# Layer-norm statistics in a Mamba, gated-linear-attention and soft-MoE stack: moved behind a step's scans and onto ScalarE, and into the last layer's loop

## The chip, the cores and the metric

The kernel runs on one core of a Trainium2 chip. A core has five engines that run at the same time, each through its own instruction queue in order: PE (TensorE, matrix products; PEld is its weight load), DVE (VectorE), ACT (ScalarE), POOL (GpSimd) and SP (SyncE, here only for starting DMAs). They wait for each other through semaphores. The metric is the device time of one execution in microseconds; less is better.

## The reference

The input is x of shape (4, 1024, 128), which is 4096 tokens of 128 numbers. Six layers are applied, each on a layer norm of x and each added back to x:

```python
x = x + 0.5 * moe(layernorm(x))        # 8 experts, top 2, capacity 1024
x = x + mamba(layernorm(x))            # 256 channels, 16 states, scan over 1024 steps
x = x + 0.5 * moe(layernorm(x))        # the same weights again
x = x + 0.5 * soft_moe(layernorm(x))   # 64 experts x 32 slots
x = x + gla(layernorm(x))              # gated linear attention, 16 heads of 8
x = x + 0.5 * soft_moe(layernorm(x))   # the same weights again
```

with

```python
def layernorm(x):
    m = mean(x, -1); v = var(x, -1)
    return (x - m) / sqrt(v + 1e-5)
```

In the Mamba layer, for every channel d and state n, `h[t] = exp(delta[t,d]*A[d,n]) * h[t-1] + delta[t,d]*B[t,n]*u[t,d]` and `y[t,d] = sum over n of h[t]*C[t,n]`; then `y = (y + u*D) * silu(z)` and the output is `y @ W_out`. In the soft layer, logits of tokens against 2048 slots are taken through a softmax within each expert (32 slots, to gather tokens into slots) and through one across experts (64, to give the slots' results back to the tokens).

## The kernel before, in words

x stays in on-chip memory all the time, as 32 tiles of 128 tokens x 128 numbers, all f32. Each of the six layer norms has three small arrays with one entry per token: mv (mean and variance), rstd and nmr. A tile is normalised by one ACT instruction, rstd * x + nmr (`ln_apply`, L156). What that needs is made in two parts. `ln_stats` takes, for a group of four tiles, a BATCH_NORM_STATS2 (L121) and a BATCH_NORM_AGGREGATE (L122) per tile on DVE, and one add of the epsilon to the variance (L125). `ln_root` raises the result to the power -1/2 on POOL (`ln_pow`, L135) and multiplies it with minus the mean on DVE (`ln_minus`, L142).

**The Mamba layer** handles four sequences in two halves of 512 tokens, one half after the other, and within a half 16 states; one state of one half is a step k of the loop. The order on each engine within the loop is that in which the code emits it (a manual schedule). A step k emits: the next instruction group of the finished half's `epilogue` (behind); `fetch` of the B and C rows for step k+3 (a DMA for ten of the 16 states, a PE broadcast, L658, for the other six; a DMA of C for four states at a time); `scan` of step k, two DVE scans of 512 tokens (L686); `keep`, on ACT, of the end state of a first half (L697); `decay` of step k+2, two ACT exponentials (L676); `times_c` of step k-1, the product hc of the state with C on POOL (L702); `feed` of step k+2, the product dBu, on POOL or on DVE (L668); `sums` of step k-2, four PE instructions that add hc into py (L717). Then come the next groups of the `prologue` of the coming half (normalisation, transposes L548, convolution L569, projections L575 and L587, Silu with table loads L580, and the softplus with DVE work at L627 to L631). hc has three buffers, dA four (two steps), the PE broadcast of B one.

A finished half's epilogue begins at step 2 of the next half: `zs` (L724, DVE) multiplies the gate with py, which `sums` of state 15 completes; two steps on, sixteen PE instructions make po (L730); one step on, DVE adds po to x (L736); one step on, `ln_stats` of the four tiles for the next layer norm.

**The second MoE layer** begins with the normalisation of all tiles (after `ln_root` over 16 tiles, twice) and with loads of the expert weights.

**The two soft layers** (`soft_bounded`) go in a first loop over 64 steps (32 tiles x 2 halves of the slots): logits on PE (L926), their minimum on DVE (L930), exponential on ACT (L935), sums of 32 and a reciprocal on DVE (L942, L943), a product on POOL (L947), a product with the tokens on PE (L958). In steps 0 to 3 of every eight, ACT normalises the next four tiles; in step 4 PE turns them (L912) and ACT takes them over (L917). The turn uses one of the two logits buffers. The second loop makes the exponentials the other way round (L1037, L1047), sums them on POOL (L1055) and mixes (L1071, L1081). In the first of these layers, `others` runs pieces of the MoE combination, with the layer norm's statistics, one piece per step of the first loop; in the last layer it is empty.

**The gated linear attention** (`gla_layer`) between them handles eight groups of 512 tokens with four steps each: PE spreads v (L1499), DVE multiplies with k (L1505) and scans (L1516), POOL multiplies with q (L1524), PE sums (L1538); an epilogue per group (L1547 to L1576) ends with an addition to x on DVE (L1576) and `ln_stats` of the group's four tiles for the last soft layer. After all eight, `ln_root` over 16 tiles runs twice. Work outside of a manual schedule is placed by the framework's planner.

Of the kernel before, what the change touches and what calls it, by code (L numbers as in the profile page):

```python
# [8 lines left out]
F32 = mybir.dt.float32  # L9
# [59 lines left out]
def macaron_kernel(ctx: ExitStack, tc: tile.TileContext, a: dict, out: bass.AP):  # L69
# [76 lines left out]
    def ln_root(ln, j0, n=4):  # L146
        ln_pow(ln, j0, n)
        ln_minus(ln, j0, n)

    def ln_group(ln, j0):  # L150
        ln_stats(ln, j0)
        ln_root(ln, j0)

    def ln_apply(dst, j, ln):
        _, rstd, nmr = ln
# [332 lines left out]
    def mamba_layer(ln, ln_next, first):  # L488
# [4 lines left out]
        with ExitStack() as s:  # L493
# [227 lines left out]
            def epilogue(r):  # L721

                zs = r["zs"]
                nc.vector.tensor_tensor(zs, zs, r["py"], ALU.mult)  # L724
                yield
                yield
                po = ps.tile([P, NJ, D], F32, name="po", tag="mm")
                for i in range(NJ):
                    for c in range(NC):
                        nc.tensor.matmul(  # L730
                            po[:, i, :], zs[:, c, i * P : (i + 1) * P], w_out[:, c, :],
                            start=(c == 0), stop=(c == NC - 1),
                        )
                yield
                jj = r["b"] * (S // P) + r["h"] * NJ
                nc.vector.tensor_tensor(  # L736
                    x[:, jj : jj + NJ, :], x[:, jj : jj + NJ, :], po, ALU.add
                )
                yield
                ln_stats(ln_next, jj, NJ)  # L740
                yield


# [8 lines left out]
            with tc.manual_schedule(engines=ENGINES):  # L752
                bring, pieces = first
                for j in range(0, 16, 4):
                    bring(j)
                run(pieces(0))


                others = (_ for j in range(4, NT, 4) for _ in pieces(j))
                for _ in prologue(*halves[0], rs[0], psa, "dA"):  # L760
                    for _ in range(3):
                        next(others, None)
                run(others)
                for k in range(3):
                    at(fetch, k)
                at(feed, 0)
                at(feed, 1)
                at(decay, 0)
                at(decay, 1)
                LEAD = 5  # L770
                ahead, old, behind = (iter(()) for _ in range(3))
                for k in range(-LEAD, len(units) + 7):
                    if k % DS == DS - LEAD and (k + LEAD) // DS + 1 < len(rs):
                        i = (k + LEAD) // DS + 1
                        old, ahead = ahead, prologue(*halves[i], rs[i])
                    if k < 0:
                        next(ahead, None)
                        continue
                    if k > DS and k % DS == 2:
                        behind = epilogue(rs[k // DS - 1])  # L780
                    next(behind, None)
                    at(fetch, k + 3)
                    at(scan, k)
                    at(keep, k)
                    at(decay, k + 2)
                    at(times_c, k - 1)
                    at(feed, k + 2)
                    at(sums, k - 2)
                    next(old, None)
                    next(ahead, None)  # L790
# [75 lines left out]
        nc.vector.tensor_copy(smod, sm0.unsqueeze(1).to_broadcast([P, 4, PS]))  # L866
        return smod

    def soft_bounded(phiN, phiM, pbc, ew, eb, tag, ln, first=None, after=None, last=False):

# [10 lines left out]
        with ExitStack() as s:  # L881
# [223 lines left out]
            with tc.manual_schedule(engines=ENGINES):  # L1105
# [6 lines left out]
                    norm(i)  # L1112
                turn(0)
                take(0)
                others = iter(())
                if first:
                    run(pieces(4))
                    others = (_ for j in range(8, NT, 4) for _ in pieces(j))
                for k in range(NK + CS * NB + XL + 3):
                    next(others, None)  # L1120
                    if k < NK:
# [262 lines left out]
    def gla_layer(ln, ln_next):  # L1384
        with ExitStack() as s:
# [158 lines left out]
            def epilogue(u):  # L1544
# [31 lines left out]
                nc.vector.tensor_tensor(  # L1576
                    x[:, u * NJ : (u + 1) * NJ, :], x[:, u * NJ : (u + 1) * NJ, :], py, ALU.add
                )
                ln_stats(ln_next, u * NJ)
                yield  # L1580


# [68 lines left out]
    def after(j):  # L1651
        ln_group(lns[4], j)
# [2 lines left out]
    with tc.If(bounded > 0) as cmp:  # L1655
        def soft(*a_, **k_):
            soft_bounded(phiN, phiM, pbc, ew, eb, *a_, **k_)
        with tc.tile_pool(name="yb", bufs=2) as yp:
            soft("a", lns[3], combine(yp, gates[1], lns[3]), after)
        behind_soft(soft)  # L1660
    with cmp.Else():
        def soft(*a_, **k_):
            soft_layer(phiN, ew, eb, *a_, **k_)
# [82 lines left out]
```

## Time and profile before

| | us |
|---|---|
| median of 3 runs (2297.42 to 2300.35) | 2300.21 |
| the profiled execution | 2299.02 |
| its span, first to last instruction | 2297.1 |
| Mamba loop (first to last scan) | 304 to 834 |
| first soft layer, first loop, about | 1096 to 1336 |
| GLA, about | 1613 to 1797 |
| last soft layer, first loop, about | 1801 to 2026 |
| statistics of one group in the Mamba on DVE (398.96 to 401.36) | 2.40 |
| BATCH_NORM_STATS2 / AGGREGATE, mean of 192 | 0.277 / 0.192 |
| pow of 4 / of 16 columns on POOL | 1.01 / 2.90 |

How to read the lines: "L686 DVE" is line 686 of the kernel before, on VectorE. A row of the timeline gives start (us from the span's start), duration, engine, line, operation, output<-input, size and count of instructions merged; in brackets stands the idle time of that engine just before it and what ended the wait. Rows of a table by stage give the window, its length, busy time (with count) of PE, PEld, DVE, ACT and POOL, the granted PE clock as a share of full speed, the share of the DMA engines and GB/s. PE's busy time holds modelled ends of pipelined products.

### The profile page before, as it was taken

Reading aid. Unit: us, or ns where it says so; the run is one execution under the profiler, and the core shown is the slowest. Engines: PE = TensorE matmul, PEld = TensorE weight load, DVE = VectorE, ACT = ScalarE, POOL = GpSimd, SP = SyncE. Lnnn points to the kernel's source line nnn. Section 1 sums busy time; section 2 is a strip of 40 time slices with the busy share of each in tenths; the row PEclk is TensorE's granted clock in tenths of the full one; section 3 lists DMA queues with packets and bytes.
Section 4 is the critical chain, followed back from the end, with each engine's and each line's share of the span. In section 5 each row is a group of like instructions: output and inputs, shape, how many; then the busy total and the mean of one; then the engine's idle time right before and its main releaser. Section 6 shows DMA issues by size and latency. Waiting matters only on the chain. (4 is left out here: it accounts for less than half of the span.)

```text
span 2297.1 us, 17954 instructions
## 1 busy us (share of the span) xinstructions
PE 1931.9 (84%) x5889; PEld 903.0 (39%) x5889; DVE 1418.5 (62%) x1947; ACT 928.1 (40%) x1453; POOL 1400.0 (61%) x904
## 2 busy tenths in 40 slices
PE   4688568888988855886899989998888899989998
PEld 3466223333333314554344444443232344434443
DVE  4311578888888955111788745556888677754444
ACT  3222365566655523222444334332543333334331
POOL 2677267888988961777455556664444455556663
PEclk9999778999989885898999999999987899999999
DMA  7111333233323332112100000000000000000000
GB/s 248 35 52 51 105 126 107 92 116 93 104 90 106 115 142 78 51 51 64 37 19 0 0 1 0 1 0 6 1 1 0 0 0 0 1 1 5 10 10 15
DMA packets 63677, 111.23 MB, mean 48 GB/s; under 512 B 7999, under 2 KB 41423, under 8 KB 58581
## 3 DMA queue, kind: packets, MB, share of 16 engines
q1 hardware_dynamic: 45062, 81.37, 10.8%
q0 software_dynamic: 8192, 16.79, 2.6%
q10 hardware_dynamic: 10322, 11.85, 1.6%
q8 instruction: 48, 0.79, 0.1%
q14 instruction: 53, 0.43, 0.1%
HBM read 90.53 MB, written 19.44 MB: 48 GB/s over the span
## 5 line engine op out<-in xcount | busy, mean ns | idle before, releaser
L947 POOL TENSOR_TENSOR dm<-ex,sm 128x1024 f32<-128x1024 f32 x128 | 247.6, 1935 | 214.5 <-DVE sm L943 117.7
L702 POOL TENSOR_TENSOR hc<-hst,Cs 128x1024 f32<-128x1024 f32 x128 | 289.2, 2271 | 77.2 <-DVE hst L686 73.6
L717 PE MATMUL py<-hc,ident 128*128 128x512 f32 x512 | 278.9, 676 | 46.0 <-POOL hc L702 46.0
L1055 POOL TENSOR_TENSOR acc<-acc,L 128x1024 f32<-128x1024 f32 x96 | 225.9, 2354 | 116.5 <-ACT L L1047 115.8
L1047 ACT ACTIVATE L<-pl,pbc 128x512 f32<-128x512 f32 x256 | 162.1, 684 | 284.0 <-PE pl L1037 273.5
L926 PE MATMUL l<-phiT,xT 128*128 128x512 f32 x512 | 247.1, 607 | 18.5 <-ACT ex L935 15.2
L935 ACT ACTIVATE ex<-l,nmh 128x1024 f32<-128x1024 f32 x128 | 142.7, 1115 | 287.7 <-DVE nmh L930 269.9
L1037 PE MATMUL pl<-xT,phiM 128*128 128x512 f32 x512 | 244.1, 601 | 0.0
L1081 PE MATMUL py<-L,yt 128*128 128x512 f32 x512 | 238.4, 593 | 4.4 <-DVE L L1071 4.4
L958 PE MATMUL px<-dm,xn 128*128 128x512 f32 x512 | 240.8, 593 | 1.1 <-POOL dm L947 1.1
L676 ACT ACTIVATE dA<-delta,A 128x512 f32<-128x512 f32 x256 | 179.2, 721 | 95.1 <-DVE hst L686 90.0
L930 DVE TENSOR_REDUCE nmh<-l 128x1 f32<-128x1024 f32 x128 | 156.5, 1223 | 87.9 <-PE l L926 87.1
L717 PEld LDWEIGHTS py<-hc,ident 128*128 128x128 f32 x512 | 97.4, 204 | 204.2 <-issue 115.2
L389 ACT ACTIVATE hT<-ph,cols 128x512 f32<-128x512 f32 x128 | 88.0, 687 | 214.6 <-PE ph L385 214.6
L668 POOL TENSOR_TENSOR dBu<-du,Bs 128x1024 f32<-128x1024 f32 x80 | 171.8, 2149 | 0.6 <-ACT dA L676 0.6
L686 DVE TENSOR_TENSOR_SCAN hst<-dA,carry,dBu 128x512 f32<-128x512 f32 x128 | 154.2, 1261 | 5.6 <-POOL dBu L668 5.6
L926 PEld LDWEIGHTS l<-phiT,xT 128*128 128x128 f32 x512 | 97.6, 194 | 149.8 <-issue 116.9
L942 DVE TENSOR_REDUCE sm<-ex 128x32 f32<-128x1024 f32 x128 | 154.7, 1209 | 0.0
L686 DVE TENSOR_TENSOR_SCAN hst<-dA,dBu 128x512 f32<-128x512 f32 x128 | 146.6, 1201 | 7.6 <-POOL dBu L668 7.5
L404 DVE TENSOR_TENSOR eo<-po,b 128x512 f32<-128x512 f32 x32 | 22.1, 692 | 207.4 <-PE po L399 207.4
L363 POOL DMA_INDIRECT y_d<-eo,dest x128 | 125.8, 982 | 35.6 <-issue 25.6
L1071 DVE TENSOR_TENSOR L<-L,rd 128x1024 f32<-128x1024 f32 x128 | 147.1, 1213 | 0.1
(248 smaller groups left out, 2976.2 us busy)
## 6 DMA issues: line engine op xcount, KB each, us to landing
Cs<-bc_d SPq DMA_DIRECT2D x32, 1024.0 KB, 4.7
Bs<-bc_d SPq DMA_DIRECT2D x80, 256.0 KB, 3.3
w<-in_w SPq DMA_DIRECT2D x4, 2048.0 KB
y<-y_d SPq DMA_DIRECT2D x32, 256.0 KB, 3.3
y_d<-zero SPq DMA_DIRECT2D x1, 4096.0 KB
ew<-in_ew ACTq DMA_DIRECT2D x1, 4096.0 KB
x<-in_x SPq DMA_DIRECT2D x8, 256.0 KB, 7.6
xn_da<-xn ACTq DMA_DIRECT2D x8, 256.0 KB, 6.9
```

The lines of the kernel that those rows point to most:

```text
L668: eng.tensor_tensor(dBu, r["du"], r.pop(("B", n)).unsqueeze(2).to_broadcast([P, HB, NC]), ALU.mult,)
L676: nc.scalar.activation(dA, r["delta"][:, :, c], AF.Exp, scale=A[:, c * DS + n : c * DS + n + 1],)
L686: nc.vector.tensor_tensor_scan(hst[:, :, c], r.pop(("dA", n, c)), dBu[:, :, c], 0.0 if h == 0 else carry[b][:, c, n : n + 1], ALU.mult, AL ...
L702: nc.gpsimd.tensor_tensor(hc, r.pop(("h", n)), Cs.unsqueeze(2).to_broadcast([P, HB, NC]), ALU.mult)
L717: nc.tensor.matmul(r["py"][:, c, :], ident, hc[:, :, c], start=False, stop=(n == DS - 1))
L926: nc.tensor.matmul(l[:, q * 512 : (q + 1) * 512], xT[:, j * P : (j + 1) * P], phiN[:, o : o + 512], start=True, stop=True,)
L947: nc.gpsimd.tensor_tensor(dms[k], exs.pop(k), sms.pop(k).unsqueeze(2).to_broadcast([P, NG, PS]), ALU.mult,)
L958: nc.tensor.matmul(px[hf * 2 + q], xns[j // 4][:, j % 4, :], dmf[:, q * 512 : (q + 1) * 512], start=(j == 0), stop=(j == NT - 1),)
L1037: nc.tensor.matmul(pl[:, i, :], phiM[:, (2 * c + i) * P : (2 * c + i + 1) * P], xT[:, t * TB : (t + 1) * TB], start=True, stop=True,)
L1047: nc.scalar.activation(L[:, i, :], pl[:, i, :], AF.Exp, bias=pbc[:, 2 * c + i : 2 * c + i + 1], scale=-1.0,)
L1055: nc.gpsimd.tensor_tensor(accs[t], accs[t], L, ALU.add)
L1081: nc.tensor.matmul(pys[t], yt[:, 2 * c + i, :], L[:, i, :], start=(c + i == 0), stop=(c == CS - 1 and i == 1),)
```

## The change

Three things change.

1. In the Mamba's loop, the finished half's next group is emitted after the step's scans, no longer at the step's head. Its statistics are made by `ln_stats_act`: four ACT Copy instructions that also accumulate the sum of a tile, one that scales the sums to minus the mean, four ACT Square instructions with that as bias that accumulate the squares, and one that scales these to the variance plus epsilon. They write a throw-away tile `junk`. The root of this layer norm is `ln_root_pool`: the pow and the multiplication with minus the mean are both on POOL.
2. In the GLA, only the first two groups (tiles 0 to 7) still have `ln_stats`, and one `ln_root` over these eight tiles follows.
3. The last soft layer takes the statistics of tiles 8 to 31 in its first loop, as `others`, in eight pieces per group of four tiles: in steps 1 and 2 of eight the statistics, in step 3 the pow, in step 5 the product.

The other branch (`cmp.Else`, another form of the soft layer that this input doesn't take) runs these pieces at once.

```diff
+    def ln_stats_act(ln, j0, n=4):
+        mv, rstd, nmr = ln
+        js = slice(j0, j0 + n)
+        junk = small.tile([P, D], F32, name="junk")
+        for j in range(j0, j0 + n):
+            nc.scalar.activation(junk, x[:, j, :], AF.Copy, accum_out=mv[:, j, 0:1])
+        nc.scalar.activation(nmr[:, js], mv[:, js, 0], AF.Copy, scale=-1.0 / D)
+        for j in range(j0, j0 + n):
+            nc.scalar.activation(
+                junk, x[:, j, :], AF.Square, bias=nmr[:, j : j + 1], accum_out=mv[:, j, 1:2]
+            )
+        nc.scalar.activation(
+            rstd[:, js], mv[:, js, 1], AF.Identity, bias=eps_t, scale=1.0 / D
+        )
+
+    def ln_root_pool(ln, j0, n=4):
+        _, rstd, nmr = ln
+        js = slice(j0, j0 + n)
+        nc.gpsimd.tensor_tensor(
+            rstd[:, js], rstd[:, js], half_t.to_broadcast([P, n]), ALU.pow
+        )
+        nc.gpsimd.tensor_tensor(nmr[:, js], nmr[:, js], rstd[:, js], ALU.mult)
+
+    def ln_pieces(ln, j):
+        yield
+        ln_sums(ln, j, 2)
+        yield
+        ln_sums(ln, j + 2, 2)
+        ln_eps(ln, j)
+        yield
+        ln_pow(ln, j)
+        yield
+        yield
+        ln_minus(ln, j)
+        yield
+        yield
+        yield
...
@@ mamba_layer, epilogue @@
-                ln_stats(ln_next, jj, NJ)
+                ln_stats_act(ln_next, jj, NJ)
...
@@ mamba_layer, loop @@
-                    next(behind, None)
                     at(fetch, k + 3)
                     at(scan, k)
+                    next(behind, None)
                     at(keep, k)
                     at(decay, k + 2)
...
@@ soft_bounded, before the first loop @@
-                others = iter(())
                 if first:
                     run(pieces(4))
-                    others = (_ for j in range(8, NT, 4) for _ in pieces(j))
+                else:
+                    pieces = rest
+                others = (_ for j in range(8, NT, 4) for _ in pieces(j))
...
@@ gla_layer, epilogue @@
-                ln_stats(ln_next, u * NJ)
+                if u < 2:
+                    ln_stats(ln_next, u * NJ)
...
     for j in range(0, NT, 16):
-        ln_root(lns[2], j, 16)
+        ln_root_pool(lns[2], j, 16)
...
     def behind_soft(soft):
         gla_layer(lns[4], lns[5])
-        for j in range(0, NT, 16):
-            ln_root(lns[5], j, 16)
-        soft("b", lns[5], last=True)
+        ln_root(lns[5], 0, 8)
+        soft("b", lns[5], rest=lambda j: ln_pieces(lns[5], j), last=True)
```

More of the change, by code (lines that the diff above doesn't have):

```diff
@@ L867, in group_sum, with soft_bounded @@
         return smod
-    def soft_bounded(phiN, phiM, pbc, ew, eb, tag, ln, first=None, after=None, last=False):
+    def soft_bounded(phiN, phiM, pbc, ew, eb, tag, ln, first=None, rest=None, after=None, last=False):
         TB = 512
@@ L1658, in macaron_kernel @@
         with tc.tile_pool(name="yb", bufs=2) as yp:
-            soft("a", lns[3], combine(yp, gates[1], lns[3]), after)
+            soft("a", lns[3], combine(yp, gates[1], lns[3]), after=after)
         behind_soft(soft)
@@ L1662, in soft @@
         def soft(*a_, **k_):
+            rest = k_.pop("rest", None)
+            if rest:
+                for j in range(8, NT, 4):
+                    run(rest(j))
             soft_layer(phiN, ew, eb, *a_, **k_)
```

## The prediction

> **What bounds the kernel now.** I read the page first (busy shares), then a table by stage, then the three stages that the change touches, instruction by instruction.
>
> ```profile
> PE 1931.9 (84%) x5889; PEld 903.0 (39%) x5889; DVE 1418.5 (62%) x1947; ACT 928.1 (40%) x1453; POOL 1400.0 (61%) x904
> ```
>
> ```profile
> 372.00:438.00 66.00, 57.07 (x128) 22.02 (x126) 56.59 (x52) 39.33 (x55) 54.83 (x26) 0.92 0.33 105
> 1637.00:1660.00 23.00, 20.08 (x84) 6.75 (x84) 21.85 (x29) 12.54 (x19) 12.31 (x6) 1.00 0.00 0
> 1830.00:1858.00 28.00, 27.63 (x68) 12.28 (x67) 21.57 (x24) 10.92 (x13) 14.96 (x8) 1.00 0.00 1
> ```
>
> The columns of the three rows below the page's line are the window, its length, busy us of PE, PEld, DVE, ACT and POOL, then clock, DMA share and GB/s. The whole-kernel 62% for DVE says little. In a Mamba half (first row) PE, DVE and POOL are each busy 83 to 86% and ACT 60%: none is the bound for the whole half, they take turns. In the GLA (second row) DVE is at 95%. In the soft layer's first loop (third row) PE is at 99% and DVE at 77%.
>
> How the turns go in one Mamba half, from the timeline:
>
> ```profile
> 385.07 1.22 DVE L724 TENSOR_TENSOR zs<-zs,py 128x1024 f32<-128x1024 f32 x1 [6.00 <-PE py L717]
> ...
> 395.99 0.69 DVE L736 TENSOR_TENSOR x<-x,po 128x512 f32<-128x512 f32 x1 [1.51 <-PE po L730]
> ...
> 400.66 0.79 DVE L125 TENSOR_SCALAR rstd<-mv 128x4 f32<-128x4 f32 x1
> ```
>
> ```profile
> 388.83 2.13 POOL L702 TENSOR_TENSOR hc<-hst,Cs 128x1024 f32<-128x1024 f32 x1 [4.69 <-DVE hst L686]
> ...
> 403.98 2.13 POOL L702 TENSOR_TENSOR hc<-hst,Cs 128x1024 f32<-128x1024 f32 x1 [2.56 <-DVE hst L686]
> ```
>
> I write scan(n), hc(n), sums(n) for state n of the half. DVE stands 6.00 us before zs, because zs needs the previous half's sums(15), and it stands there in front of scan(2); POOL then waits 4.69 us for scan(2) to make hc(2). Six of the eight zs have this wait (5.99 to 6.00 us), the one in the last half has none, the eighth lies behind the loop. The statistics (398.96 to 401.36, 2.40 us) stand in front of scan(6), and POOL waits 2.56 us for it. From hc(6) to 428 us POOL has no gap, and DVE waits for it (0.88 us at 418.71): there POOL is the bound.
>
> **The change, part by part.** The sum is made on the profiled execution: 2299.0 us, of which the span is 2297.1.
>
> *Mamba, pieces behind the scans.* scan(2) goes ahead of zs. Its inputs are there: dBu(2) left POOL at 377.6 and dA(2) and dA(3) ACT before 378.8, so it runs 379.0 to 381.5 within the old wait. zs does not move, since the end of its wait is PE's sums(15) at 385.03, behind the next half's convolution in PE's queue, and PE's order of instructions is the same in both programs. So scan(3) starts at 386.2 in place of 388.6: 2.4 us. The add L736 now follows scan(5); its 1.51 us wait for po shrinks to about 0.6.
>
> *Mamba, statistics on ScalarE.* DVE loses 2.40 us per half. DVE then runs scan(3), scan(4), dBu(6), scan(5) from 386.2 to 394.6, the add to 395.9, and ends scan(6) at 398.4 in place of 403.8: DVE is 5.4 us earlier. POOL can't take all of it. hc has three buffers, so hc(6) needs sums(3) done, and PE has no slack there: from 386.35 to 397.7 it runs back to back (sums(2) starts at 395.79), then a 1.1 us broadcast, then sums(3), which I put at an end of 400.2 to 400.5. hc(6) so starts at about 400.5, not 403.98: 3.5 us. The same walk through the half at 441 gives 468.5 against 471.86: 3.4 us. Behind it POOL is dense, so its lead is kept to the half's end, and DVE and ACT, which lead by more, follow.
>
> ACT gets eight accumulating activations and two short ones per half. None exists in this trace. Nearest rows: a scaled 128x128 Copy 389 ns (L454), a 128x128 with a bias pointer 365 ns (L1560), a 128x2 Copy 190 ns (L697), and a dependent pair (L620, L622) 0.04 us apart: 4 x 0.39 + 4 x 0.37 + 2 x 0.19 + 10 x 0.04 = 3.8 us. [...] Queued behind it on ACT are dA(8), and the copy of dbc, for which PE's delta product waits. With dA(7) out at 397.9 the pieces end at 401.7, dA(8) at 403.2, scan(8) at 405.0; DVE is ready for scan(8) at 402.0 and gets its first input at 402.5, so it loses half a microsecond, hidden: hc(8) stood at 412.35 and now stands at 408.9. This cover holds until the ten take about 7.3 us. [...] No table load is added.
>
> Seven halves have an epilogue behind them. Six gain 3.4; the last, without the zs wait and with one POOL wait of 0.47, gains 0.5: -20.9.
>
> *POOL's pow and product.* The pow over 16 columns (2.90 us) stands in half 4. Before, it lay in a hole: hc(6) came 5.09 us after hc(5) there, 4.56 in other even halves, so it cost 0.5. Now it stands behind dBu(9), in the dense stretch, with a product of some 0.2: +2.6. The second pair at the end is hidden: the tiles that need it are normalised after 874, and ACT's own chain there (statistics, a 1.90 us copy, four expert-bias issues in between: done near 854) lies under the wait for weights that holds ACT until 860.22. If those weights came earlier, up to 7 us would show. The expert-bias DMAs go out some 4 us later, but on the same queue behind a 4 MB load.
>
> *GLA.* Six of eight groups of statistics (1.8 us each, 10.9 in all) leave DVE. At 95% this looks like 10.9 us. But:
>
> ```profile
> 1663.40 0.63 ACT L1551 ACTIVATE sq<-og 128x512 f32<-128x512 f32 x1
> ...
> 1664.44 1.13 PE L1499 MATMUL pv<-qkv,spread_w 32*128 32x512 f32 x4
> ...
> 1665.68 1.23 DVE L1505 TENSOR_TENSOR pv<-pv,qkv 128x1024 f32<-128x1024 f32 x1
> ...
> 1787.59 0.68 DVE L1547 SCALAR_TENSOR_TENSOR og<-po,fg 128x512 f32<-128x512 f32 x1
> ```
>
> After a group at 1657.5 to 1659.3, DVE's second product from there (1665.68) starts 0.1 us after PE's 1664.44 matmuls end, and these wait on ACT's square, which stands behind a copy of PE's own result (ended 1663.42). PE has no gap from 1653.4 to 1662.8. So 1.8 us of DVE time turns into a wait for PE: nothing gained in the loop. At the end one counts: the 1787.59 line waits only for the statistics ahead of it, PE was done at 1786.0: -1.5. At the seam the first min-reduce (1804.78) stood behind a pow-and-multiply pair: -0.3. Ends for this part: 0 and -11. The clock is an unknown too: the granted clock is 1.00 in some GLA windows and 0.57 from 1751 to 1800. [...]
>
> *Last soft layer.* It takes six groups of statistics (0.8 us in each of two steps, then the eps add, a 1.0 us pow on POOL, a 0.1 us product). The first soft layer shows the price of such pieces:
>
> ```profile
> 1173.10 1.28 DVE L125 TENSOR_SCALAR rstd<-mv 128x4 f32<-128x4 f32 x1
> ...
> 1176.77 1.98 PE L926 MATMUL l<-phiT,xT 128*128 128x512 f32 x4 [1.65 <-ACT ex L935]
> ...
> 1817.88 1.98 PE L926 MATMUL l<-phiT,xT 128*128 128x512 f32 x4 [0.37 <-ACT ex L935]
> ```
>
> There the eps add stretched to 1.28 us beside POOL in the step that also turns a tile group, where both logits buffers are taken, and PE stood 1.28 us longer (1.65 against 0.37 without pieces): 7.7 us for six. In the new order the sums fall in steps 1 and 2 of 8 and the turn in step 4. DVE has 0.70 us spare per step: late by 0.1 after step 1, by at most 1.5 after step 2, and back to about 0 after step 4's reduce. So +0.3 in all, with 0 and +7.7 as ends.
>
> Sum: -20.9 + 2.6 - 1.5 - 0.3 + 0.3 = -19.8; 2299.0 becomes 2279.2. The runs' median is 2300.2, 1.2 above the profiled one: 2280.4, say **2280**.
>
> **Rivals.** A: *PE does not hold POOL back* (sums keep up because the hc arrive earlier), so DVE's 5.4 us pass on: 6 x 2.0 = 12 more, 2268; with part of the GLA's 10.9, down to 2258. Against it: PE's row of 57.07 in 66. B: *a part is given back*, by statistics of 7 to 9 us on ACT or by the soft layer's 7.7: 2287 to 2295. C: *PE sets the half's pace throughout*, and the change does not do what it says: DVE and POOL wait for sums later, only the 0.7 us that PE waits for ACT at 389.99 goes, 6 x 0.7 - 2.6 + 1.8: within 4 us, 2297. Against it: PE waits 2.3 us for POOL at 434.19, so it catches up within the half. D, *slower*: the accumulating activations are long. Between dA(7) and dA(8), each microsecond above 7.3 delays scan(8), then POOL, by one in seven halves; 3.5 us more eat the gain, so it decides from 10.8 us, or 1.25 us per activation, over three times the nearest row. At 1.6 us the ten take 13.6: 7 x 2.8 + 1 above, 2321.
>
> **How the numbers follow.** Likeliest 0.45 (its own range 2274 to 2287), A 0.17, B 0.18, C 0.09, D 0.11. The three runs before spread by 0.13%, so 0.2% (4.6 us) is about what a measurement tells from nothing. Faster: the likeliest, A and B, 0.80; same: C, 0.09; slower: D, 0.11. The range leaves out D, most of C and A's far end: 2262 to 2296.
>
> **What would show it.** Right: the wait before zs near 3.5 us, with scan(2) ahead of it; no POOL wait for scan(2); hc(6) 15.4 us after zs starts in place of 18.9; ten ACT pieces near 3.8 us in all; PE stalls of 0.4 us at the last layer's turns; GLA length less 1.5 only. Wrong: hc(n) waiting for PE more than I allow (C), a DVE wait for dA before scan(8) over 3 us (D), or GLA halves shorter than 19.3 us (A).

## The result, and the profile after

| | before | after |
|---|---|---|
| median | 2300.28 us (6 runs, 2297.42 to 2307.24) | 2275.64 us (6 runs, 2273.84 to 2278.42) |
| ratio after / before | | 0.9890, 95% interval 0.9875 to 0.9906 |
| the profiled execution, its span | 2299.02, 2297.1 us | 2274.64, 2272.9 us |

The kernel is faster by 1.1%, 24.6 us; 2280 was predicted. The lines of the two programs differ: 686 became 727 (scan), 702 became 743 (hc), 717 became 758 (sums), 724 became 765 (zs), 736 became 777 (the addition to x). I again write scan(n), hc(n) and sums(n). The page's busy shares of after, and three rows of its table by stage (window, length, busy us of PE, PEld, DVE, ACT, POOL, then clock, DMA share, GB/s), for the windows that answer to those shown before:

```profile
PE 1914.3 (84%) x5889; PEld 894.6 (39%) x5889; DVE 1404.0 (62%) x1878; ACT 954.6 (42%) x1597; POOL 1404.5 (62%) x911
```

```profile
371.26:437.26 66.00, 57.65 (x131) 22.20 (x130) 58.09 (x46) 44.22 (x76) 58.39 (x27) 0.94 0.34 105
1618.80:1641.80 23.00, 20.08 (x84) 6.74 (x84) 21.85 (x29) 12.49 (x19) 12.36 (x6) 1.00 0.00 0
1805.50:1833.50 28.00, 27.63 (x68) 12.25 (x67) 23.97 (x34) 10.91 (x13) 15.85 (x9) 1.00 0.00 1
```

In the Mamba half ACT has 4.9 us more, and POOL 3.6 us more in the same 66 us: POOL is fuller because it stands less. The GLA row in the middle of its loop is the same as before. The soft row has 2.4 us more of DVE and the same PE.

The sum by stage, from the starts of the same instructions in both traces:

| stage (us) | before | after | difference | predicted |
|---|---|---|---|---|
| start to the first zs | 385.07 | 384.33 | -0.74 | 0 |
| first zs to last zs (Mamba) | 454.94 | 437.24 | -17.70 | -18.3 |
| last zs to the GLA's first spread of v | 773.36 | 773.63 | +0.27 | 0 |
| that to the GLA's last addition to x | 183.22 | 174.63 | -8.59 | -1.5 |
| that to the first logits of the last soft layer | 4.34 | 4.34 | 0 | -0.3 |
| that to the last computing instruction | 492.12 | 494.17 | +2.05 | +0.3 |

The differences add up to -24.71; the two profiled executions differ by -24.38. The Mamba came out as forecast. Two small terms of the sum did not: the GLA gave 7.1 us more, and the last soft layer took 1.8 us more. The seam's -0.3 did not come either: the first minimum starts 3.82 us behind the first logits (3.85 before), because DVE now waits there for PE's logits.

The timeline of after, DVE and POOL at the head of the same half:

```profile
378.25 2.45 DVE L727 TENSOR_TENSOR_SCAN hst<-dA,carry,dBu 128x512 f32<-128x512 f32 x2
384.33 1.22 DVE L765 TENSOR_TENSOR zs<-zs,py 128x1024 f32<-128x1024 f32 x1 [3.64 <-PE py L758]
...
384.43 2.13 POOL L743 TENSOR_TENSOR hc<-hst,Cs 128x1024 f32<-128x1024 f32 x1 [1.00 <-POOL dBu L709]
...
389.53 2.13 POOL L743 TENSOR_TENSOR hc<-hst,Cs 128x1024 f32<-128x1024 f32 x1 [0.87 <-PE py L758]
393.43 2.14 POOL L743 TENSOR_TENSOR hc<-hst,Cs 128x1024 f32<-128x1024 f32 x1 [1.77 <-PE py L758]
...
400.06 2.13 POOL L743 TENSOR_TENSOR hc<-hst,Cs 128x1024 f32<-128x1024 f32 x1 [0.30 <-PE py L758]
...
403.09 4.81 DVE L727 TENSOR_TENSOR_SCAN hst<-dA,carry,dBu 128x512 f32<-128x512 f32 x4 [1.43 <-ACT dA L717]
```

scan(2) now runs inside the wait for zs, which shrinks from 6.00 to 3.64 us. hc(2) no longer waits 4.69 us for it. POOL's waits at hc(3), hc(4) and hc(6) are now for PE's sums, and hc(6) starts 15.73 us behind zs in place of 18.91. The last line of the timeline is a new wait: DVE stands 1.43 us for dA(8), which lies behind the statistics on ACT.

### The profile page after: what moved, and what is told of

Its sections match the earlier page's. It is cut to its first block, busy times and chain, and to the rows that moved or that the text cites. A ratio compares the mean times of both kernels' runs of the same rounds, so it can differ in the third digit from the quotient of the medians.

```text
span 2272.9 us, 18043 instructions
## 1 busy us (share of the span) xinstructions
PE 1914.3 (84%) x5889; PEld 894.6 (39%) x5889; DVE 1404.0 (62%) x1878; ACT 954.6 (42%) x1597; POOL 1404.5 (62%) x911
## 5 line engine op out<-in xcount | busy, mean ns | idle before, releaser
L758 PE MATMUL py<-hc,ident 128*128 128x512 f32 x512 | 271.4, 658 | 47.8 <-POOL hc L743 47.5
L968 PE MATMUL l<-phiT,xT 128*128 128x512 f32 x512 | 248.0, 609 | 18.6 <-ACT ex L977 15.4
L1123 PEld LDWEIGHTS py<-L,yt 128*128 128x128 f32 x512 | 96.8, 190 | 127.3 <-issue 117.0
```

What stands on the lines that cost most here:

```text
L758: nc.tensor.matmul(r["py"][:, c, :], ident, hc[:, :, c], start=False, stop=(n == DS - 1))
L968: nc.tensor.matmul(l[:, q * 512 : (q + 1) * 512], xT[:, j * P : (j + 1) * P], phiN[:, o : o + 512], start=True, stop=True,)
L1123: nc.tensor.matmul(pys[t], yt[:, 2 * c + i, :], L[:, i, :], start=(c + i == 0), stop=(c == CS - 1 and i == 1),)
```

## The experiments

Times are set against the kernel before (2300.44, 2301.20 and 2299.15 us in the three groups of runs below). The medians are of 4 runs, of 14 for the ACT statistics alone and the GLA and soft part alone, of 12 for the statistics twice, of 6 for after. The last three columns are read from one trace each: first to last zs; the GLA from its first spread of v to its last addition to x; from there to the last computing instruction. What lies ahead of the first zs is in the medians only. It differs from trace to trace (376.7 to 387.0 us), by 4.7 us even among four kernels whose programs are the same up to there (384.33 in the changed kernel, 383.49, 380.90 and 379.63 in those with one root, three groups and five groups). So a difference of a few us between two medians says little, and the columns say more.

| kernel | median us | ratio to before, 95% | zs to zs | GLA | rest |
|---|---|---|---|---|---|
| before | 2300.28 | | 454.94 | 183.22 | 496.46 |
| after | 2275.64 | 0.9890 (0.9875 to 0.9906) | 437.24 | 174.63 | 498.51 |
| order alone | 2282.32 | 0.9907 (0.9872 to 0.9942) | 436.81 | 182.01 | 497.30 |
| ACT statistics alone | 2293.03 | 0.9970 (0.9953 to 0.9986) | 449.27 | 183.19 | 496.53 |
| both Mamba parts | 2280.97 | 0.9904 (0.9870 to 0.9938) | 437.29 | 183.37 | 496.51 |
| GLA and soft part alone | 2293.00 | 0.9963 (0.9950 to 0.9977) | 454.86 | 174.53 | 498.51 |
| four hc buffers | 2265.53 | 0.9850 (0.9825 to 0.9876) | 430.07 | 174.66 | 498.44 |
| one root of 32 columns | 2271.55 | 0.9882 (0.9857 to 0.9907) | 434.11 | 174.78 | 498.18 |
| three GLA groups keep statistics | 2273.29 | 0.9891 (0.9865 to 0.9916) | 437.39 | 174.64 | 498.43 |
| five groups keep them | 2272.07 | 0.9887 (0.9861 to 0.9912) | 437.27 | 177.08 | 495.91 |
| ACT statistics twice | 2295.59 | 0.9990 (0.9977 to 1.0003) | 460.95 | 174.65 | 497.25 |
| version for use, ACT | 2256.16 | 0.9828 (0.9794 to 0.9862) | 425.57 | 177.00 | 496.07 |
| the same, DVE statistics | 2274.79 | 0.9897 (0.9866 to 0.9929) | 437.21 | 175.10 | 497.56 |

### Which part of the change earns the Mamba's gain

The order alone, against the changed kernel (the GLA and the last soft layer as before):

```diff
-                ln_stats_act(ln_next, jj, NJ)
+                ln_stats(ln_next, jj, NJ)
-        ln_root_pool(lns[2], j, 16)
+        ln_root(lns[2], j, 16)
-                if u < 2:
-                    ln_stats(ln_next, u * NJ)
+                ln_stats(ln_next, u * NJ)
-        ln_root(lns[5], 0, 8)
-        soft("b", lns[5], rest=lambda j: ln_pieces(lns[5], j), last=True)
+        for j in range(0, NT, 16):
+            ln_root(lns[5], j, 16)
+        soft("b", lns[5], rest=lambda j: iter(()), last=True)
```

> Only the order is changed: in the Mamba loop the finished half's pieces come behind the step's scans; its statistics stay on DVE and their root stays as it was, and the GLA and the last soft layer are as before. Theory 1 (PE's sums hold POOL at hc(6), as the prediction says): the order alone already brings scan(6) ahead of what hc(6) can take, so hc(6) comes about 3.4 us earlier per half and the statistics, now behind scan(6), cost DVE 2.4 us that POOL does not see; first to last zs shorter by 18 to 20 us, less up to 2.6 if the pow lands in a dense stretch: -16 to -20 in all. Theory 2 (each part earns the wait that it removes, and they add up): only the wait at zs goes, 6 x 2.4 = 14.4 us less the pow: -12 to -14. Theory 3 (the statistics behind scan(6) now hold scan(7), and POOL pays there): -5 or less.

The ACT statistics alone (the GLA and the soft layer as before in the same way):

```diff
-                    at(fetch, k + 3)
-                    at(scan, k)
                     next(behind, None)
+                    at(fetch, k + 3)
+                    at(scan, k)
```

> Only the statistics are changed in the Mamba: on ScalarE, with the root and its product on POOL; the pieces still come at the head of the step, and the GLA and the last soft layer are as before. Theory 1 (PE's sums hold hc(6)): the wait at zs stays, hc(2) is as late as before, and only the 2.40 us in front of scan(6) go, seven times: -17, plus 2.6 for the pow: about -14; together with the order alone this is far more than both parts at once, so the two share one wait. Theory 2 (they add up): what both give less what the order gives, that is -4 to -6. Theory 3 (the ten ACT pieces hold back scan(8) as much as DVE gains): 0 to -3.

Both Mamba parts, with only the GLA and the soft layer undone:

```diff
-                if u < 2:
-                    ln_stats(ln_next, u * NJ)
+                ln_stats(ln_next, u * NJ)
-        ln_root(lns[5], 0, 8)
-        soft("b", lns[5], rest=lambda j: ln_pieces(lns[5], j), last=True)
+        for j in range(0, NT, 16):
+            ln_root(lns[5], j, 16)
+        soft("b", lns[5], rest=lambda j: iter(()), last=True)
```

> Both Mamba parts of the change; the GLA and the last soft layer are as before. By the two traces the Mamba gives 17.7 to 18.4 us and the moe layer and the first soft layer behind it nothing: -18. If the GLA's gain is the clock's, moved by the earlier start, then the GLA is shorter here too, by up to 8.6: -18 to -27. If it is the statistics', the GLA keeps its 183 us.

Measured from zs to zs: the order alone 436.81, both 437.29, the ACT statistics alone 449.27. So the order gives -18.1, the statistics alone -5.7, and both together no more than the order. The timeline of the order alone, the half at 387, DVE's rows and below them POOL's hc(5) and hc(6):

```profile
386.98 1.22 DVE L765 TENSOR_TENSOR zs<-zs,py 128x1024 f32<-128x1024 f32 x1 [3.64 <-PE py L758]
...
398.37 2.45 DVE L727 TENSOR_TENSOR_SCAN hst<-dA,carry,dBu 128x512 f32<-128x512 f32 x2
400.74 0.27 DVE L121 BATCH_NORM_STATS2 st<-x 128x6 f32<-128x128 f32 x1
...
402.44 0.17 DVE L125 TENSOR_SCALAR rstd<-mv 128x4 f32<-128x4 f32 x1
...
400.27 2.14 POOL L743 TENSOR_TENSOR hc<-hst,Cs 128x1024 f32<-128x1024 f32 x1
402.70 2.14 POOL L743 TENSOR_TENSOR hc<-hst,Cs 128x1024 f32<-128x1024 f32 x1 [0.29 <-DVE rstd L125]
```

The statistics now stand behind scan(6), which is done at 400.8, when POOL has only just begun hc(5) (400.27). hc(6) starts at 402.70, 15.72 us behind zs, as in the changed kernel. (The 0.29 us are put down to the statistics' last instruction, which hc(6) doesn't read; in the changed kernel the same 0.30 us stand there for PE's sums.) The 1.9 us of statistics lie in time that DVE has ahead of POOL. This is theory 1. With the order changed, moving the statistics to ScalarE earned nothing in the Mamba; between single zs the two kernels differ by up to 1.6 us, both ways.

The ACT statistics alone were expected at -14 by theory 1 and gave -5.7, near theory 2's figure but not for its reason. The timeline of PE in that run's second interval between zs, and its rows by stage, show why:

```profile
467.69 3.76 PE L758 MATMUL py<-hc,ident 128*128 128x512 f32 x8
473.40 1.16 PE L656 MATMUL pd<-dbc,w_dt 8*128 8x512 f32 x1 [1.95 <-ACT dbc L633]
...
475.35 3.78 PE L758 MATMUL py<-hc,ident 128*128 128x512 f32 x4
```

```profile
469.00:473.40 4.40, 2.45 (x6) 0.75 (x5) 2.04 (x3) 4.24 (x16) 4.40 (x3) 1.00 0.24 56
473.40:479.00 5.60, 5.60 (x8) 1.61 (x8) 5.60 (x7) 5.28 (x11) 3.76 (x2) 0.51 0.51 130
479.00:487.00 8.00, 8.00 (x10) 2.99 (x10) 5.71 (x6) 5.80 (x10) 6.24 (x3) 0.50 0.34 117
```

The statistics push ACT's copy of dbc back; PE's delta product waits 1.95 us for it, with later sums behind it in PE's queue. Then PE's granted clock is 0.50 for over 13 us, and four sums take 3.78 us where the unhindered ones take half of that (eight in 3.76). From zs to zs this took 68.42 us against 68.51 before, so it gained nothing; the interval ahead of it, without this stop, gained 2.6 (65.02 against 67.60). The stop of 1.95 us comes in the second, the fourth and the sixth interval (at 473.40, 608.38 and 742.88), and these three gained 0.1 and 0.1 us and lost 1.5. The first, the third and the fifth, without it, gained 2.6, 1.1 and 2.4: there the 2.40 us of statistics were in part or wholly earned, as theory 1 has it.

### The GLA and the last soft layer

The third part alone:

```diff
-                ln_stats_act(ln_next, jj, NJ)
+                ln_stats(ln_next, jj, NJ)
-        ln_root_pool(lns[2], j, 16)
+        ln_root(lns[2], j, 16)
-                    at(fetch, k + 3)
-                    at(scan, k)
                     next(behind, None)
+                    at(fetch, k + 3)
+                    at(scan, k)
```

> Only the third part: the GLA without its statistics from the third group on, these taken in the last soft layer; the Mamba is as before. By the prediction's terms -1.5. By the two traces, if the statistics are the cause of all that the GLA lost: -8.6 in the GLA, +2.2 at the head of the last soft layer, -6.4 in all. If 2.7 us of the GLA's gain (the interval between the fifth and the sixth group's addition to x, where only the fall of PE's clock came later) hang on when the GLA starts: -3.7.

The GLA takes 174.53 us here and 183.37 with the Mamba parts alone. With all eight groups' statistics the GLA takes 182.0 to 183.4 us in four traces, with two or three groups' 174.5 to 174.8 in six. So the sum of 8.6 us comes with the statistics, not with when the GLA starts, and all of the 2.05 us at the end of the program comes with it (498.51). The intervals between the eight additions to x locate it: before 19.34, 23.27, 24.34, 21.06, 24.17, 16.06, 11.54; after 19.34, 23.25, 24.34, 20.79, 21.43, 13.30, 8.72. The first four change by 0.3 us in all; the last three lose 2.74, 2.76 and 2.82 us.

Timeline of DVE in the kernel before, from the sixth addition on:

```profile
1768.99 0.68 DVE L1576 TENSOR_TENSOR x<-x,py 128x512 f32<-128x512 f32 x1
1769.70 0.29 DVE L121 BATCH_NORM_STATS2 st<-x 128x6 f32<-128x128 f32 x1
...
1771.51 2.44 DVE L1516 TENSOR_TENSOR_SCAN st<-fg,st,pv 128x512 f32<-128x512 f32 x2
1773.87 1.21 DVE L1505 TENSOR_TENSOR pv<-pv,qkv 128x1024 f32<-128x1024 f32 x1
```

The same place in the kernel after:

```profile
1747.81 0.68 DVE L1619 TENSOR_TENSOR x<-x,py 128x512 f32<-128x512 f32 x1
1748.41 2.45 DVE L1559 TENSOR_TENSOR_SCAN st<-fg,st,pv 128x512 f32<-128x512 f32 x2
1750.77 1.21 DVE L1548 TENSOR_TENSOR pv<-pv,qkv 128x1024 f32<-128x1024 f32 x1
```

From the addition to the scan it was 2.52 us and is 0.60. No longer wait for PE follows to take the 1.92 us back, as one did at 1665: DVE's next wait for PE is 2.23 us in both, and there is no prologue of a next group any more to fill PE. The last interval has the 1.5 us that were predicted (the og of the last group started 2.54 us behind the addition, and now 1.00). What is left of the three, about 4.9 us, goes with PE's clock. Two rows by stage of before, and the two at the same distance from the GLA's start of after:

```profile
1752.00:1758.00 6.00, 5.23 (x22) 1.52 (x23) 4.13 (x5) 4.04 (x6) 2.53 (x2) 0.67 0.00 0
1758.00:1764.00 6.00, 5.78 (x17) 2.35 (x17) 4.30 (x5) 0.02 (x1) 2.34 (x1) 0.50 0.00 0
```

```profile
1733.80:1739.80 6.00, 5.32 (x32) 2.01 (x24) 4.12 (x4) 3.77 (x5) 2.19 (x1) 0.96 0.00 0
1739.80:1745.80 6.00, 5.79 (x18) 2.47 (x16) 4.66 (x5) 0.00 (x0) 3.21 (x2) 0.50 0.00 0
```

The clock falls to 0.50 in both, but about 3 us later in the new kernel, and the products for the gates (four in 2.07 us before, 1.13 after) then still run at full speed.

Two variants ask which statistics matter, and whether the first pieces in the last soft layer cost its head:

```diff
-                if u < 2:
+                if u < 3:            # second kernel: 5
-        ln_root(lns[5], 0, 8)
+        ln_root(lns[5], 0, 12)       # second kernel: 20
-                others = (_ for j in range(8, NT, 4) for _ in pieces(j))
+                lead = 0 if first else 4     # second kernel: 12
+                others = (_ for j in range(8 + lead, NT, 4) for _ in pieces(j))
-                    next(others, None)
+                    if k >= 2 * lead:
+                        next(others, None)
```

> The changed kernel with the statistics of the first three groups in the GLA, and the last soft layer's pieces from the fourth group on, which start eight steps later. The statistics of the third group lie where the GLA's loop has PE as its bound. If the loop up to the fifth group does not feel DVE's statistics, the GLA stays at 174.6 us from its first spread of v to its last addition to x; and if the first pieces, in steps 1 and 2, are what costs the head of the last soft layer, its first turn of tiles comes 17.0 us behind its first logits, not 19.19: -2.2. Rival: the head is late for PE's clock (cold behind the GLA's shorter end), not for the pieces: 19.2 stays, 0.

> The changed kernel with the statistics of the first five groups in the GLA, and the pieces from the sixth group on. Theory 1 (only the statistics behind the last prologue count directly; the shorter interval between the fifth and the sixth addition is the clock's, set off by the statistics of the fifth group): the last two intervals stay at 13.3 and 8.7, the one before them goes back from 21.43 to about 24.1: GLA 177.3, +2.7 against the changed kernel, less up to 2.2 at the head of the last soft layer. Theory 2 (the shorter intervals come from the lead that all groups before have gathered): the last intervals go back too, 16.1 and 11.5, GLA near 183.

With five groups the interval before the last two goes back to 24.19, and the last two stay short (11.83 and 9.63, a sum of 21.5 against 27.6 before and 22.0 after): theory 1, that only the statistics behind the last prologue count directly and the rest is when the clock falls. But the statistics alone do not decide when it falls, those of the fifth group, which the expectation named, as little as others. The two last versions below have the same program in the GLA and the last soft layer, with the first four groups' statistics, and differ there. The row by stage of the version with ScalarE, and the one at the same distance from the GLA's start of that with DVE:

```profile
1716.30:1722.30 6.00, 5.31 (x22) 1.66 (x23) 2.66 (x3) 4.00 (x5) 2.35 (x1) 0.67 0.00 0
```

```profile
1736.00:1742.00 6.00, 5.32 (x30) 2.16 (x32) 3.92 (x4) 3.96 (x5) 2.35 (x1) 0.96 0.00 0
```

The interval from the fifth to the sixth addition is 24.03 us in the first and 21.68 in the second. The traces of all thirteen kernels fall into these two kinds: it is 24.0 to 24.2 us where the clock had been back at 1.00 for 13.7 us when it fell (before and five groups among them), and 21.4 to 21.7 where it had been so for 17.1 us (after and three groups). The order alone, with all eight groups' statistics, is of the second kind: its last three intervals are 21.73, 14.10 and 11.53, so 4.4 of the 8.3 us are gone there with no statistics moved (its first interval is 3.0 us longer instead, at a clock that fell early). What moves the fall from one kind to the other stays open.

At the head of the last soft layer, the logits behind the first turn of tiles come 19.19 us behind the first logits in the changed kernel, 17.87 with three groups (17.0 were expected without the pieces), 16.62 with five, 16.95 before. The changed kernel's timeline there shows the pieces of step 2 in front of a minimum that PE's next logits need:

```profile
1783.60 0.23 DVE L121 BATCH_NORM_STATS2 st<-x 128x6 f32<-128x128 f32 x1
...
1784.48 1.31 DVE L125 TENSOR_SCALAR rstd<-mv 128x4 f32<-128x4 f32 x1
1785.71 1.21 DVE L972 TENSOR_REDUCE nmh<-l 128x1 f32<-128x1024 f32 x1
```

So 1.3 us of the loss at the turn go when the pieces start eight steps later. The rest is PE's clock. The rows for the first 8 us from the first logits of before, three groups, the changed kernel and the third part alone:

```profile
1800.93:1808.93 8.00, 7.57 (x12) 2.91 (x12) 4.03 (x8) 3.60 (x4) 2.90 (x1) 0.73 0.00 0
```

```profile
1770.69:1778.69 8.00, 8.00 (x12) 3.28 (x12) 2.46 (x3) 2.74 (x3) 0.00 (x0) 0.62 0.00 0
```

```profile
1774.17:1782.17 8.00, 8.00 (x12) 3.27 (x12) 3.19 (x7) 2.74 (x3) 0.00 (x0) 0.62 0.00 1
```

```profile
1796.20:1804.20 8.00, 7.25 (x13) 2.92 (x14) 4.47 (x9) 4.15 (x5) 0.00 (x0) 0.82 0.00 0
```

The clock is still at 0.50 for the first 4.35, 6.11, 6.16 and 2.85 us of these. In the kernels without pieces in the head the place of the turn follows this time: 16.62 us at 3.62 (five groups), 16.95 at 4.35 (before), 17.53 at 5.50 (order alone), 17.87 at 6.11 (three groups), half a us for each us of it. On this line the changed kernel would stand at 17.9 and the third part alone at 16.2; they stand at 19.19 and 17.75, 1.3 and 1.5 us behind it. So, as an estimate from these traces, of the 2.24 us at the turn 1.3 are the pieces' and 0.9 the clock's. With three groups the program's rest was no shorter (498.43), since its second loop was some 1.3 us longer. In that trace and in that of the third part alone the clock falls to 0.50 for 3.41 us three times within the first 40 us of that loop, in the changed kernel's twice.

### Whether PE's sums hold POOL through the buffers

```diff
-                dBu = r["dBu", n] = wk.tile([P, HB, NC], F32, name="dBu")
+                dBu = r["dBu", n] = wk.tile([P, HB, NC], F32, name="dBu", bufs=3)
-                hc = r["hc", n] = wk.tile([P, HB, NC], F32, name="hc", bufs=3)
+                hc = r["hc", n] = wk.tile([P, HB, NC], F32, name="hc", bufs=4)
```

> The changed kernel with four buffers for hc in place of three; to make room the dBu tile has three in place of four, which costs no wait, since POOL makes dBu(n) behind hc(n-3), which needs scan(n-3) anyway. Theory 1 (PE's sums hold POOL through the number of hc buffers): POOL's waits of 0.87 and 1.77 us for py at hc(3) and hc(4) go, hc(6) then comes when scan(6) is out, about 13.8 us behind zs in place of 15.73, and each of six halves is 1.5 to 1.9 us shorter: -9 to -12 against the changed kernel. Theory 2 (PE sets the pace of the half itself, the buffers only show it): hc(6) moves, and PE, or the wait of 3.6 us for hst near the half's end, takes it back: 0 to -3.

From zs to zs 430.07, 7.2 us less than the changed kernel. The timeline of POOL with four buffers:

```profile
387.68 2.14 POOL L743 TENSOR_TENSOR hc<-hst,Cs 128x1024 f32<-128x1024 f32 x1 [0.32 <-DVE hst L727]
390.12 2.13 POOL L743 TENSOR_TENSOR hc<-hst,Cs 128x1024 f32<-128x1024 f32 x1 [0.30 <-DVE hst L727]
...
397.96 2.14 POOL L743 TENSOR_TENSOR hc<-hst,Cs 128x1024 f32<-128x1024 f32 x1 [1.14 <-DVE hst L727]
```

The waits for py are gone, and hc(6) comes 14.01 us behind zs, when scan(6) lets it: theory 1's place, which shows the step that held POOL to 3.5 us. The sum is smaller than -9 to -12: the first and third intervals between zs are 2.9 us shorter (61.49), the second only 0.8 (64.21), because POOL there waits 4.7 us for hst later in the half, and the fifth is 1.3 us longer (65.72).

### What the pow costs

```diff
-    for j in range(0, NT, 16):
-        ln_root_pool(lns[2], j, 16)
+    ln_root_pool(lns[2], 0, NT)
```

> The changed kernel with one pow and one product of 32 columns behind the whole Mamba in place of two of 16. Prediction's term: the first pair stands in POOL's dense stretch in the fifth half and costs 2.6 us there; the pair at the end is hidden under the wait for the expert weights, also at 32 columns (about 5.5 us of pow): the fifth half's length falls from 68.17 to about 65.1 (the difference of the third and the fifth half in the changed kernel is 3.11), zs to zs 437.24 to 434.2, and nothing behind it moves: -2.6 to -3.1. Rival: the 32 columns come out too late for the first normalised tiles, the weights no longer hide it: 0 to +3.

The half that held the pow falls from 68.17 to 65.04 us, zs to zs from 437.24 to 434.11, and from the last scan to the GLA nothing changes (782.1 us, after 782.0): -3.1, as said. The second pow, also at 32 columns, is hidden.

### How far ScalarE's cover reaches

```diff
                 ln_stats_act(ln_next, jj, NJ)
+                ln_stats_act(ln_next, jj, NJ)
```

> The changed kernel with the ten ACT statistics instructions of a half issued twice over, so 8.6 us in place of the 4.3 measured. Theory 1 (the prediction's cover: POOL does not feel ScalarE's statistics until they take 7.3 us; above that, one for one in seven halves): scan(8) comes 4.3 us later, 1.4 to 1.7 us too late for hc(8): first to last zs 437.24 becomes 446 to 449, +9 to +12. Theory 2 (the copy of dbc and the exponentials behind the statistics are already on the path, as the new waits of 1.4 and 1.9 us of DVE for dA suggest): the whole 4.3 us in each half, +26 to +30. Theory 3 (cover to the half's end): 0 to +2.

From zs to zs 460.95: +23.7, about twice theory 1's figure and below theory 2's. The timelines of PE and POOL:

```profile
407.26 1.21 PE L656 MATMUL pd<-dbc,w_dt 8*128 8x512 f32 x1 [3.30 <-ACT dbc L633]
...
409.27 3.78 PE L758 MATMUL py<-hc,ident 128*128 128x512 f32 x4
...
408.78 2.14 POOL L743 TENSOR_TENSOR hc<-hst,Cs 128x1024 f32<-128x1024 f32 x1 [1.59 <-DVE hst L727]
413.19 2.13 POOL L743 TENSOR_TENSOR hc<-hst,Cs 128x1024 f32<-128x1024 f32 x1 [2.27 <-PE py L758]
```

hc(8) waits 1.59 us for scan(8), as theory 1 has it (1.4 to 1.7). But the next hc waits 2.27 us more, for sums that PE could not start: PE stood 3.30 us for the copy of dbc, and then ran at a granted clock of 0.50 (from 407.2 to 413.0), so that four sums took 3.78 us in place of 2.06. The prediction named this copy in ACT's queue and then priced only dA(8). PE stands 3.3 to 3.6 us for it in all six intervals where the loop makes a next half. With 8.6 us of statistics the Mamba's whole gain is lost.

### Together

```diff
-                dBu = r["dBu", n] = wk.tile([P, HB, NC], F32, name="dBu")
+                dBu = r["dBu", n] = wk.tile([P, HB, NC], F32, name="dBu", bufs=3)
-                hc = r["hc", n] = wk.tile([P, HB, NC], F32, name="hc", bufs=3)
+                hc = r["hc", n] = wk.tile([P, HB, NC], F32, name="hc", bufs=4)
-    for j in range(0, NT, 16):
-        ln_root_pool(lns[2], j, 16)
+    ln_root_pool(lns[2], 0, NT)
-                if u < 2:
+                if u < 4:
-        ln_root(lns[5], 0, 8)
+        ln_root(lns[5], 0, 16)
-                others = (_ for j in range(8, NT, 4) for _ in pieces(j))
+                lead = 0 if first else 8
+                others = (_ for j in range(8 + lead, NT, 4) for _ in pieces(j))
-                    next(others, None)
+                    if k >= 2 * lead:
+                        next(others, None)
```

> A version for use: the changed kernel with four hc buffers (dBu three), one root of 32 columns behind the Mamba, and the GLA's statistics kept in its loop for the first four groups. The single runs gave -7.2 and -3.1 us from first to last zs for the first two, and nothing in sum for where the split of the statistics lies. If they add: zs to zs 426.9, and about 10 us less than the changed kernel, 2263 to 2266.

2256.16 us, 0.9828 of the kernel before (0.9794 to 0.9862), an interval below the changed kernel's (0.9875 to 0.9906): faster than both; zs to zs 425.57, 1.4 us less than if the two single gains add up. The median is below the 2263 to 2266 that were expected, for a reason that is not shown: of the 18.0 us between the two profiled executions 11.7 lie between the zs and 7.6 ahead of the first one, where kernels with the same program differ by 4.7. The GLA is 2.4 us longer and the rest 2.4 us shorter than in the changed kernel, so the split of the statistics was worth nothing there either.

The same with the Mamba's statistics on DVE:

```diff
-                ln_stats_act(ln_next, jj, NJ)
+                ln_stats(ln_next, jj, NJ)
-    ln_root_pool(lns[2], 0, NT)
+    ln_root(lns[2], 0, NT)
```

> The same as the version with four hc buffers, one root and four groups, but the Mamba's statistics on DVE behind the scans (the root on POOL and its product on DVE). Theory 1 (with three buffers ScalarE's statistics bought nothing because POOL stood for PE; with four POOL stands 1.1 us for DVE's scan(6), so 2.4 us of DVE behind it are felt at hc(7)): first to last zs 1.5 us longer in six halves, about 436, +9 against the version with ScalarE. Theory 2 (the wait for dA, which only ScalarE's statistics cause, is worth the same, and POOL's two products between give DVE the time): equal, within 2 us.

2274.79 us, zs to zs 437.21: 11.6 us longer than with ScalarE. The timeline of POOL with DVE's statistics and four buffers:

```profile
397.23 2.13 POOL L743 TENSOR_TENSOR hc<-hst,Cs 128x1024 f32<-128x1024 f32 x1 [1.14 <-DVE hst L727]
...
403.05 2.13 POOL L743 TENSOR_TENSOR hc<-hst,Cs 128x1024 f32<-128x1024 f32 x1 [1.59 <-DVE hst L727]
```

hc(7) is 1.59 us late behind DVE's statistics (theory 1 had 1.5), a wait that the run with ScalarE does not have. So what ScalarE's statistics are worth depends on the buffers of another tile: nothing with three, about 12 us with four. And the fourth buffer is worth nothing without them: 437.21 us here, against 436.81 with the order alone and three.

## Why the prediction was right, and where not

*Right, the Mamba.* The steps held nearly to the number: the wait before zs 3.64 us (3.5 predicted), scan(2) inside it, hc(6) 15.73 us behind zs (15.4), zs to zs -17.7 (-18.3). Four buffers showed the reason that was given, PE's sums through the three hc buffers; with four, rival A's premise, that PE doesn't hold POOL back, becomes true at hc(6) and brings 7.2 of its 12 us. The pow's +2.6 measured +3.1 against no pow; that half gained 1.3 us where its neighbours gained 3.2. The sixth half and the last were priced at 3.4 and 0.5 and gave 1.1 and 2.3: two misses that by luck nearly cancel.

*Right in sum, wrong in its account: "Mamba, statistics on ScalarE".* The walk had DVE 5.4 us earlier and let POOL take 3.5, without asking whether the first part alone already reaches that limit. It does: as changed, the move neither gained the Mamba time nor lost it (zs to zs 437.29 us for both parts, 436.81 for the order alone); it pays only with four buffers (425.57 against 437.21).

*Mis-sized, ScalarE's price and cover.* The ten pieces took 4.3 us, not 3.8: each of the eight accumulating activations (0.31 or 0.40 us) is followed by an instruction that reads the accumulator, 0.19 us. "So it loses half a microsecond" at scan(8) was 1.43 to 1.93 us; it was hidden, as said. The cover "until the ten take about 7.3 us", and with it rival D's 10.8 us, looked only at dA(8): at 8.6 us the gain was already gone, with PE standing 3.3 to 3.6 us for the copy of dbc six times and the clock at 0.50 behind it each time.

*Failed, "GLA tail -1.5".* The mechanism that makes DVE's time worthless, a dense PE, ends with the last prologue, one group earlier than the term had it. Another 1.9 us count there, and 4.9 us more went with PE's clock, which the prediction named as an unknown and gave no term in its sum; how much of these the statistics cause stays open, since the order alone has 4.4 us of them without moving any. "GLA length less 1.5 only" was therefore wrong; "nothing gained in the loop" was right for the four intervals up to the fifth addition.

*Mis-sized, "last soft layer +0.3".* In the steady loop it holds: PE stands 0.37 us at the turns, the period is 28.54 us before and after. The recovery by step 4 supposes a pipeline that is running; in the first eight steps it is not. There the pieces cost about 1.3 us and PE's clock about 0.9, by the estimate above, and the program's rest grew by 2.05 us. The sum had no term for the clock in this layer.

The predicted 2280 missed by 4.4 us: the GLA's 7.1 less the 1.8 of the last soft layer, and small terms around the Mamba. So two misses partly cancel in the number.

## What to carry to other kernels

When two edits each remove a wait from the same chain, find the limit behind both (here the buffer count of a third tile) before adding them up; here, once the first edit was in, neither the second nor the raised limit earned anything alone in the Mamba, and the two together did. Work that was free inside a loop because another engine was dense was not free in the loop's last rounds and first rounds (1.9 us from the addition to the scan in the GLA's last rounds, about 1.3 us at the head of the last soft layer): price these rounds on their own. For work put into an engine's queue, price everything behind it, above all what another engine's queue waits for in order (here the copy of dbc, for which PE stood 3.3 to 3.6 us in the run with the ACT statistics twice).

## What the runs showed of the hardware

In the run with the ACT statistics alone a wait of PE of 1.95 us was followed by a granted clock of 0.50 for over 13 us (473.4 to 487), in which PE was busy all the time, and after it 1.00 again. The length of the stop does not decide this: the same 1.95 us at 608.38 and 742.88 were followed by 3.4 and 10.2 us at 0.50, and in the kernel before five of six stops of 2.5 to 2.7 us at the same product by 3.4 us and the sixth by 6.8. In the traces of the kernels before and after (90 and 78 stretches of one value) the granted clock is either 0.50 or 1.00, and each stretch but the last of a trace is a whole multiple of 3.41 us long. What makes it fall and return is not shown. In the changed kernel an accumulating activation on ScalarE over 128x128 took 0.31 us (Copy) or 0.40 us (Square with a bias column), and each was followed by its own accumulator read of 0.19 us. A DVE addition over 128x4 that took 0.17 us in the GLA took 1.28 us six times in the first soft layer before and 1.28 to 1.58 us in the last one after; at 1173.10 (before) and 1784.48 (after) a product of POOL was under way. That the product is the cause is not shown.
